# Edge selectors made from SBUF a batch ahead, and range sums turned one batch later, in a graph layer on one core

## Chip, cores and metric

One core of one Trainium2 chip. The metric is the device time of one execution in microseconds (us); lower is better.

## The reference

One layer of a graph network over 12500 nodes and 400000 edges, in fp32. Edges are sorted by destination; half of the destinations lie in the first quarter of the nodes, so at the low end a node has many edges and at the high end few.

```python
h = relu(layernorm(x))                                   # (12500, 160): 64 scalars, 32 vectors of 3
y0, y1 = h[:, :64] @ W_l1_0, einsum(h[:, 64:], W_l1_1)   # by node
w = silu(edge_attr_16 @ fc_W1) @ fc_W2                   # by edge: w_a 64, w_b 64, w_c 32, w_d 32
ys0, ys1 = y0[src], y1[src]                              # a gather of 160 numbers an edge
mid0 = concat(w_a * ys0 * e0, w_d * dot(ys1, e1) / sqrt(3))
mid1 = concat((w_b * ys0) x e1, (w_c * e0) * ys1)        # e0, e1: the 4 numbers of edge_attr_4
z = scatter_add(mid, dst)                                # sum over the edges of a node
out = x + C_S * (h @ W_sc) + C_X * (z @ W_l2)            # each scaled by node_vec1
```

## The kernel before, in words

A first phase normalises the nodes, maps them and writes y to HBM (`y_d`). The main loop then takes the 3125 tiles of 128 edges in 782 batches of four. An edge's contribution is not made out in full: VectorE makes 320 products an edge (weights times gathered row, `pr`), and the sum over edges comes from one fp32 matmul a tile, `selector^T @ pr`. The selector (`sel`) has 4 x 32 columns an edge: for each of a 32-node window it holds the edge's four e numbers where the edge ends at that node, and zero elsewhere. It is made in two steps: `own` compares a row 0..31 (`iota`) with the edge's node inside the window, and `sel` multiplies `own` by the four e numbers.

`ev` in SBUF holds five numbers an edge, the four e and the node inside the window, for a block of 96 tiles (24 batches). Before the change, ScalarE copies the batch's 20 columns of `ev` into PSUM, behind the batch's weights in the tile `pw` (`scale`, L524), and `own` (L620) and `sel` (L622) read them there.

A run of tiles that shares one 32-node window is a range. It has 24 tiles at the crowded end and 12, 8, 6, 4 and at last 3 at the other (`WTS`); 598 ranges in all, and four of them are a group. The matmuls of a range add up in one PSUM buffer `pz` (L636, two buffers). After the last one VectorE turns the sums by 32x32 blocks out of PSUM into `za` (L642, L643). Once a group is done, TensorE maps `za` by the output weights (`linear`, L649), places the rows (`add`, L661), and VectorE adds them to the result in SBUF (`accumulate`, L672).

The order on every engine is the one that the program writes (a manual schedule). In step b of the loop:

- TensorE: `weigh(b + 2)`, the weights of a later batch (L606, PSUM tile `pw`, two buffers, so it needs the products of batch b to be done); `linear` and `add` of the last group; then `sums(b)` (L636); every four steps two hidden layers (L585).
- VectorE: `products(b + 1)`, that is own (L620), sel (L622) and three multiplications (L529 and twice L533) that read `pw` and the gathered rows `yg`; then `accumulate` and some smaller work; then, inside `sums(b)`, the two turnings L642 and L643 of each range that ended in batch b.
- ScalarE: the copy L524 behind each `weigh`, and the activations.
- GpSimd: the gathers of rows (L571, an indirect DMA a tile), up to four batches ahead; a gather waits for the sums of the batch four before it ("rows keep step with the sums"). Sixteen batches get their rows from TensorE instead, without gathers.
- SyncE: loads of edge data.

`sel` has four buffers, `pr` three, `yg` six. At L720 and L723 sixteen times a pair of masks is made by VectorE from two SBUF tensors; L778 scales e numbers of those sixteen batches in place.

Of the kernel before, what the change touches and what calls it, by code (L numbers as in the profile page):

```python
# [10 lines left out]
F32 = mybir.dt.float32  # L11
I32 = mybir.dt.int32
AF = mybir.ActivationFunctionType
ALU = mybir.AluOpType
# [4 lines left out]
P = 128  # L19
M0 = 64  # L20
M1 = 32
D = M0 + 3 * M1
FC_IN = 16
FC_H = 64
NW = 2 * M0 + 2 * M1
PC = 320
ZC = 448
ZK = 5
GT = 4
BT = 32  # L30
WN = 32
# [20 lines left out]
def kernel(  # L52
# [19 lines left out]
    nc = tc.nc  # L72
# [7 lines left out]
    wts_of = [next(w for w in WTS if w == WTS[-1] or 2 * w * min((q + 1) * BLK, T) * N <= FILL * T * T)  # L80
              for q in range(NQ)]
    gstart, glist = [], []
    for q, w in enumerate(wts_of):
        gstart.append(len(glist))
        n = min(BLK, T - q * BLK)
# [3 lines left out]
    NB = (T + GT - 1) // GT  # L89
# [11 lines left out]
    iota = const.tile([P, 2 * P], F32, name="iota")  # L101
# [213 lines left out]
    def store(g, n, eng):  # L315
        node_dma(g, n, lambda rows, t, p: eng.dma_start(by_tile(out[rows, :]), acc[:p, g + t.start:g + t.stop, :]))
# [202 lines left out]
    before.close()  # L519


    def scale(pw, ev, n):

        nc.scalar.activation(pw[:, :n, NW:NW + 5], ev[:, :n, :], AF.Copy)  # L524

    def multiply(pr, wt, yg, n):

        y1 = yg[:, :n, M0:].rearrange("p t (c u) -> p t c u", c=3)
# [7 lines left out]
    with (  # L536
# [10 lines left out]
        hids, rows, wts, sels, z_ps, zT, o_sb, prs, sums_ps, summed = ({} for _ in range(10))  # L547
# [3 lines left out]
        group_of = [g for g, (_, _, n) in enumerate(glist) for _ in range(-(-n // GT))]  # L551
        first_of = [lo // GT for _, lo, _ in glist]
        assert len(group_of) == NB

        def tiles_of(b):
            return list(range(b * GT, min((b + 1) * GT, T)))

        def slots_of(b):
            n = len(tiles_of(b))
            return n if n == 1 else GT  # L560
# [38 lines left out]
        def weigh(b):  # L599
            hT = hids[b // 2]  # L600
            pw = p_w.tile([P, GT, 256], F32, name="pw")
            n = slots_of(b)
            for k in (0, 2, 1, 3):
                if k < n:
                    r, o = slice(FC_H * (k // 2), FC_H * (k // 2 + 1)), P * (b % 2 * 2 + k % 2)
                    nc.tensor.matmul(pw[:, k, 0:NW], hT[r, o:o + P], w2[r, :], start=True, stop=True)  # L606
            scale(pw, e4_of(b), n)
            wts[b] = pw

        def e4_of(b):  # L610
            o = b * GT % BLK
            return ev4[b * GT // BLK][0][:, o:o + GT, :]

        def products(b):

            n, wt, yg = slots_of(b), wts.pop(b), rows.pop(b)
            own = selp.tile([P, GT, WN], F32, name="own")
            sel = sels[b] = selp.tile([P, GT, 4, WN], F32, name="sel")[:, :n, :, :]
            pr = prs[b] = prod.tile([P, GT, PC], F32, name="pr")
            nc.vector.tensor_tensor(own[:, :n, :], iota[:, 0:WN].unsqueeze(1).to_broadcast([P, n, WN]),  # L620
                                    wt[:, :n, NW + 4:NW + 5].to_broadcast([P, n, WN]), ALU.is_equal)
            nc.vector.tensor_tensor(sel, own[:, :n, :].unsqueeze(2).to_broadcast([P, n, 4, WN]),  # L622
                                    wt[:, :n, NW:NW + 4].unsqueeze(3).to_broadcast([P, n, 4, WN]), ALU.mult)
            multiply(pr, wt, yg, n)

        def sums(b):
            pr, sel, g = prs.pop(b), sels.pop(b), group_of[b]
            q, lo, _ = glist[g]
            WT = wts_of[q]
            for k, t in enumerate(tiles_of(b)):  # L630
                w, o = divmod(t - lo, WT)
                if o == 0:
                    z_ps[g, w] = p_z.tile([P, 512], F32, name="pz")
                pz = z_ps[g, w]
                last = o == WT - 1 or t == T - 1
                mm = nc.tensor.matmul(pz[:, 0:PC], sel[:, slot(t), :, :], pr[:, slot(t), :], start=o == 0, stop=last)  # L636
                (halves if k == 1 else summed)[b] = mm.ins.name
                if last:
                    if w == 0:
                        zT[g] = post.tile([P, ZK, P], F32, name="za")  # L640
                    pz, at_w = z_ps.pop((g, w)), slice(WN * w, WN * (w + 1))
                    nc.vector.transpose(zT[g][:, :, at_w], pz[:, D:PC].rearrange("p (k u) -> p k u", k=ZK))  # L642
                    nc.vector.transpose(zT[g][0:32, :, at_w], pz[0:32, 0:D].rearrange("p (k u) -> p k u", k=ZK))  # L643

        def linear(g):
            m, za = WN * windows_of(g), zT.pop(g)
# [144 lines left out]
        weigh(0)  # L791
        if NB > 1:
            weigh(1)
        products(0)
        early = [x for x in groups if x[0] < LOW]
        assert early[-1][0] + early[-1][1] == LOW and first_of[GE] + K + len(early) <= NB
        for b in range(NB):
            g = group_of[b]
            k = b - first_of[g]
            if b + EARLY < NB:  # L800
                features(b + EARLY)
            q, r = divmod(b, KB)
            if r == 0:
                e4_load(q + 1)
            if r == KB - 4:
                e4_join(q + 1)
            u, v = divmod(b, SB)
            su, sv = divmod(b - SS, SK)
            if b + 2 < NB:
                weigh(b + 2)  # L810
            if g and 0 < k < K:
                (linear, add)[k - 1](g - 1)
            if b == SS - 8:
                skip_load(0)
            if sv in skips and 0 <= su < NU:
                skips[sv](su)
            low_pt = None
            if r == KB - 13 and q + 1 < NQ:
                low_pt = p_x.tile([MW, P], F32, name="px")[:windows_in(q + 1), :]
                turn_low(q + 1, low_pt)  # L820
            if r == KB - 11 and q + 1 < NQ:
                spread(q + 1, p_x.tile([P, MW], F32, name="px")[:, :windows_in(q + 1)])
            picked = None
            if u < XB:
                if v == 2:
                    hot_turn(u)
                elif v in (3, 6):
                    picked = look_up(u, HN * (v == 6))
                elif v == 7:
                    x_center(u)  # L830
                elif v in (9, 10):
                    x_turn(u, HN * (v == 10))
                elif v == 11:
                    x_map(u, 0)
            if v == 1 and 0 < u <= XB:
                x_map(u - 1, HN)
            if b + 1 < NB:
                products(b + 1)
            if g and k == K - 1:
                accumulate(g - 1)  # L840
            if sv == 7 and 0 <= su < NU:
                skip_add(su)
            if picked is not None:
                pick(u, HN * (v == 6), *picked)
            if v == SB - 2 and u < XB:
                x_scale(u)
            if v == 11 and u + 1 < XB:
                hot(u + 1)
            if r == KB - 15 and q + 1 < NQ:
                lowest(q + 1)  # L850
            if low_pt is not None:
                most(q + 1, low_pt)
            if r == KB - 8 and q + 1 < NQ:
                relate(rp, q + 1)
                if q + 2 == NQ:
                    any_far(rp, p_x.tile([1, 1], F32, name="px"))
            if early and b > first_of[GE] + K - 1:
                store(*early.pop(0), nc.sync)
            sums(b)
            for m, part in ((b + AHEAD - 1, slice(2, GT)), (b + AHEAD, slice(0, 2))):  # L860
                if AHEAD <= m < NB and m not in xs_of:
                    gather(m, part)
            if b % 4 == 0 and b + 4 < NB:
                hidden_pair((b + 4) // 2)
        assert SS + NU * SK <= first_of[GE] + K and NQ > 1
        for h in ([NG - 2] if NG > 1 else []) + [NG - 1]:
            for k, stage in enumerate((linear, add, accumulate)):
                if h == NG - 1 or min(k + 1, K - 1) > NB - 1 - first_of[NG - 1]:
                    stage(h)
# [5 lines left out]
    with (  # L875
# [4 lines left out]
        n = nc.values_load(far_i[0:1, 0:1], min_val=0, max_val=1)  # L880
        with tc.For_i(0, n, 1) as _:
# [8 lines left out]
            with tc.For_i(0, TP // GT, 1) as g:  # L890
# [4 lines left out]
                ev = fp.tile([P, GT, 5], F32, name="f_ev")  # L895
# [21 lines left out]
                pw = fpw.tile([P, GT, 256], F32, name="f_pw")  # L917
# [5 lines left out]
                for k in range(GT):  # L923
                    pd = fpp.tile([P, P], F32, name="f_pd")
                    nc.tensor.transpose(pd, df[:, k:k + 1].to_broadcast([P, P]), ident)
                    sel = fp.tile([P, P], F32, name="f_sel")
# [6 lines left out]
                                         scale=ev[:, k, 0:1])  # L933
                    nc.scalar.activation(ones[:, :, 0, :], low[:, M0:].rearrange("p (c u) -> p c u", c=3), AF.Copy,
                                         scale=ev[:, k, 0:1])
                    for c in range(3):
# [3 lines left out]
                                             scale=ev[:, k, 1 + c:2 + c])  # L940
# [10 lines left out]
                    pz = fpp.tile([P, ZC], F32, name="f_pz")  # L951
# [6 lines left out]
            with tc.For_i(0, NT, 1) as i:  # L958
# [4 lines left out]
                for c in range(3):  # L963
                    o = 256 + 64 * c
# [62 lines left out]
```

## Time and profile before

| | |
|---|---|
| runs | 4689.0 us median of 3 (4669.65 to 4695.63) |
| profiled execution | 4669.59 us, span 4667.7 us from the first instruction to the last |
| mean granted TensorE clock | 0.885 of full speed |
| busy | TensorE 80%, weight loads 53%, VectorE 59%, ScalarE 12%, GpSimd 63% |
| DMA | 329 MB, mean 70 GB/s |

The lines that follow come from one profiled execution. A group row has the line, the engine (PE TensorE, PEld its weight loads, DVE VectorE, ACT ScalarE, POOL GpSimd), the operation, out<-in, the shapes and the count; then busy us in all and mean ns of one; then the idle time of that engine just before these instructions, and what ended most of it ("issue": nothing that the profile shows). An fp32 matmul stands as two entries. A timeline row has start, duration, engine, line and operation, and in brackets the idle time before it and what ended it. Ends of matmuls are modelled.

### The profile page before, as it was taken

How to read it: one execution, taken by the hardware profiler on the slowest of the kernel's cores; microseconds unless marked ns; L12 is line 12 of the kernel's file. 1: busy time of each engine (PE TensorE's matmuls, PEld its weight loads, DVE VectorE, ACT ScalarE, POOL GpSimd, SP SyncE). 2: the span in 40 equal slices, each digit the busy share in tenths (PEclk: the TensorE clock that was granted, in tenths of full speed). 3: DMA queues.
4: the chain of work that ended last, by engine and by line, in shares of the span. 5: the costliest groups of instructions: out<-in, count | busy, mean ns of one | idle time of the engine just before them, and what ended most of it. 6: DMA issues, size and time to landing. Idle time of an engine off the chain costs nothing.

```text
span 4667.7 us, 53917 instructions
## 1 busy us (share of the span) xinstructions
PE 3717.5 (80%) x17202; PEld 2479.6 (53%) x17202; DVE 2735.8 (59%) x6877; ACT 580.9 (12%) x1845; POOL 2963.4 (63%) x3144
## 2 busy tenths in 40 slices
PE   7787787788877877777887788777877788888877
PEld 7455455455555554554555555555555555555545
DVE  5455555565556555555556566656556666666665
ACT  5111111111111101011101001111011110111100
POOL 5666666666666666666666666666666666666665
PEclk8888988889889888888888888988888898899998
DMA  7222222222222222222222222222222222222223
GB/s 192 69 61 64 64 65 66 65 65 64 62 64 65 69 72 62 67 69 66 68 68 67 65 71 67 68 67 67 65 70 66 68 63 64 68 67 71 63 63 113
DMA packets 262501, 329.03 MB, mean 70 GB/s; under 512 B 82888, under 2 KB 212216, under 8 KB 262216
## 3 DMA queue, kind: packets, MB, share of 16 engines
q0 software_dynamic: 150128, 256.23, 20.6%
q1 hardware_dynamic: 111590, 69.02, 5.2%
q8 instruction: 140, 2.29, 0.2%
q14 instruction: 145, 1.19, 0.1%
q10 hardware_dynamic: 498, 0.30, 0.0%
HBM read 307.67 MB, written 17.61 MB: 70 GB/s over the span
## 4 chain that ended last, share of the span: by engine, by line
PE 60%; another core or an unknown queue 13%; DVE 12%; issue 9%; ACT 2%; POOL 1%; DVEq 1%; ACTq 0%; DMA 0%; SPq 0%; POOLq 0%
PE pz L636 31%; PE pw L606 13%; PE px L649 6%; DVE pr L533 4%; PE px L585 3%; DVE pr L529 2%; PE px L661 2%; DVE za L642 1%; DVE za L643 1%; ACT hT L590 1%; POOL yg L571 1%; DVE own L620 1%; PE px L707 1%; PE px L706 1%
## 5 line engine op out<-in xcount | busy, mean ns | idle before, releaser
L571 POOL DMA_INDIRECT yg<-y_d,src_q x3061 | 2897.7, 947 | 1642.4 <-issue 803.1
L636 PE MATMUL pz<-pr,sel 128*128 128x320 f32 x6250 | 2069.0, 478 | 61.7 <-DVE za L643 39.6
L636 PEld LDWEIGHTS pz<-pr,sel 128*128 128x128 f32 x6250 | 1254.8, 211 | 607.6 <-issue 248.8
L606 PE MATMUL pw<-w,hT 64*128 64x192 f32 x6250 | 782.2, 368 | 508.3 <-DVE pr L533 276.0
L606 PEld LDWEIGHTS pw<-w,hT 64*128 64x128 f32 x6250 | 538.7, 198 | 953.3 <-issue 792.2
L642 DVE STREAM_TRANSPOSE za<-pz 128x160 f32<-128x160 f32 x598 | 205.5, 344 | 1034.8 <-PE pz L636 438.5
L533 DVE TENSOR_TENSOR pr<-pw,yg 128x384 f32<-128x384 f32 x1532 | 774.0, 547 | 0.0
L529 DVE TENSOR_TENSOR pr<-pw,yg 128x512 f32<-128x512 f32 x766 | 524.1, 684 | 192.5 <-DMA yg<-y_d,src_q 177.8
L622 DVE TENSOR_TENSOR sel<-own,pw 128x512 f32<-128x512 f32 x782 | 537.0, 687 | 27.0
L524 ACT ACTIVATE pw<-ev 128x20 f32<-128x20 f32 x782 | 149.5, 191 | 2957.7 <-PE pw L606 972.2
L649 PE MATMUL px<-wo,za 128*128 128x160 f32 x1500 | 330.7, 384 | 178.5 <-ACT hT L590 149.6
L649 PEld LDWEIGHTS px<-wo,za 128*128 128x128 f32 x1500 | 284.6, 247 | 220.1 <-ACT hT L590 165.0
L620 DVE TENSOR_TENSOR own<-iota,pw 128x128 f32<-128x128 f32 x782 | 199.6, 255 | 247.6 <-ACT pw L524 209.4
L585 PE MATMUL px<-xe,w 32*128 32x512 f32 x782 | 270.3, 658 | 63.0 <-ACT os L651 33.6
L590 ACT ACTIVATE hT<-px 128x512 f32<-128x512 f32 x391 | 220.2, 594 | 554.9 <-PE px L585 173.9
L643 DVE STREAM_TRANSPOSE za<-pz 32x160 f32<-32x160 f32 x598 | 202.2, 338 | 20.5
L672 DVE SCALAR_TENSOR_TENSOR acc<-px,a_sb,acc 128x160 f32 x300 | 114.1, 380 | 120.0 <-remote 33.6
L585 PEld LDWEIGHTS px<-xe,w 32*128 32x128 f32 x782 | 72.4, 189 | 177.7 <-issue 99.1
L661 PE MATMUL px<-os,place 128*128 128x160 f32 x600 | 133.3, 349 | 35.8 <-ACT os L651 24.2
L661 PEld LDWEIGHTS px<-os,place 128*128 128x128 f32 x600 | 94.1, 205 | 76.1 <-issue 41.7
L715 DVE SCALAR_TENSOR_TENSOR acc<-px,look,acc 128x160 f32<-128x160 f32 x98 | 33.1, 379 | 131.2 <-PE pz L636 38.3
L651 ACT ACTIVATE os<-px 128x160 f32<-128x160 f32 x150 | 44.9, 300 | 349.5 <-PE pz L636 91.2
(128 smaller groups left out, 1435.0 us busy)
## 6 DMA issues: line engine op xcount, KB each, us to landing
yg<-y_d,src_q POOLq DMA_INDIRECT x3061
xe<-in_e SPq DMA_DIRECT2D x784, 32.0 KB
xs<-in_x SPq DMA_DIRECT2D x48, 160.0 KB
acc<-in_x SPq DMA_DIRECT2D x11, 640.0 KB
y_d<-ys SPq DMA_DIRECT2D x11, 640.0 KB
out<-acc SPq DMA_DIRECT2D x11, 640.0 KB
raw<-in_e SPq DMA_DIRECT2D x32, 192.0 KB
src_q<-in_src SPq DMA_DIRECT2D x32, 48.0 KB
```

What stands on the lines that cost most here:

```text
L529: nc.vector.tensor_mul(pr[:, :n, :].rearrange("p t (x u) -> p t x u", x=2)[:, :, :, 0:M0], wt[:, :n, 0:NW].rearrange("p t (x u) -> p t x u ...
L533: nc.vector.tensor_mul(pr[:, :n, D * x + M0:D * (x + 1)].rearrange("p t (c u) -> p t c u", c=3), wt[:, :n, 96 * x + M0:96 * (x + 1)].unsqu ...
L571: fetch = nc.gpsimd.indirect_dma_start(out=yg[:, slot(t), :], out_offset=None, in_=y_d, in_offset=bass.IndirectOffsetOnAxis(ap=ev4[t // BL ...
L585: nc.tensor.matmul(ph, w1[r, :], xe[r, :], start=True, stop=True)
L590: nc.scalar.activation(hT, ph, AF.Silu, scale=1.0 / math.sqrt(FC_IN))
L606: nc.tensor.matmul(pw[:, k, 0:NW], hT[r, o:o + P], w2[r, :], start=True, stop=True)
L622: nc.vector.tensor_tensor(sel, own[:, :n, :].unsqueeze(2).to_broadcast([P, n, 4, WN]), wt[:, :n, NW:NW + 4].unsqueeze(3).to_broadcast([P, ...
L636: mm = nc.tensor.matmul(pz[:, 0:PC], sel[:, slot(t), :, :], pr[:, slot(t), :], start=o == 0, stop=last)
L642: nc.vector.transpose(zT[g][:, :, at_w], pz[:, D:PC].rearrange("p (k u) -> p k u", k=ZK))
L643: nc.vector.transpose(zT[g][0:32, :, at_w], pz[0:32, 0:D].rearrange("p (k u) -> p k u", k=ZK))
L649: nc.tensor.matmul(po[:m, :], za[:, k, :m], wo[:, k, :], start=k == 0, stop=k == ZK - 1)
L661: nc.tensor.matmul(ps[:, h, :], place[:m, h, :], os[:m, :], start=True, stop=True)
```

## The change

`scale` and its call go. A new `select(b)` makes own and sel from `ev` in SBUF; it is called for b + 2 behind `products(b + 1)`, so the selector is there a batch earlier and stands behind the products in VectorE's queue instead of before them. `own` lies in another pool, with two buffers. The turning moves out of `sums` into `leave_ranges`, which works off a list of ended ranges: it is called in step b before `sums(b)`, so that ranges that ended in batch b - 1 are turned behind `products(b + 1)` and `select(b + 2)`. Where the range after the next one starts by batch b + 1 at the latest, its PSUM buffer is wanted sooner, and the ranges are turned at once as before.

```diff
-    def scale(pw, ev, n):
-        nc.scalar.activation(pw[:, :n, NW:NW + 5], ev[:, :n, :], AF.Copy)
...
+        starts = [lo + o for q, lo, n in glist for o in range(0, n, wts_of[q])]
+        ended = []
...
-            scale(pw, e4_of(b), n)
             wts[b] = pw
...
+        def select(b):
+            n, ev = slots_of(b), e4_of(b)
+            own = post.tile([P, GT, WN], F32, name="own")
+            sel = sels[b] = selp.tile([P, GT, 4, WN], F32, name="sel")[:, :n, :, :]
+            nc.vector.tensor_tensor(own[:, :n, :], iota[:, 0:WN].unsqueeze(1).to_broadcast([P, n, WN]),
+                                    ev[:, :n, 4:5].to_broadcast([P, n, WN]), ALU.is_equal)
+            nc.vector.tensor_tensor(sel, own[:, :n, :].unsqueeze(2).to_broadcast([P, n, 4, WN]),
+                                    ev[:, :n, 0:4].unsqueeze(3).to_broadcast([P, n, 4, WN]), ALU.mult)
+
         def products(b):
             n, wt, yg = slots_of(b), wts.pop(b), rows.pop(b)
-            own = selp.tile([P, GT, WN], F32, name="own")
-            sel = sels[b] = selp.tile([P, GT, 4, WN], F32, name="sel")[:, :n, :, :]
             pr = prs[b] = prod.tile([P, GT, PC], F32, name="pr")
-            nc.vector.tensor_tensor(own[:, :n, :], iota[:, 0:WN].unsqueeze(1).to_broadcast([P, n, WN]),
-                                    wt[:, :n, NW + 4:NW + 5].to_broadcast([P, n, WN]), ALU.is_equal)
-            nc.vector.tensor_tensor(sel, own[:, :n, :].unsqueeze(2).to_broadcast([P, n, 4, WN]),
-                                    wt[:, :n, NW:NW + 4].unsqueeze(3).to_broadcast([P, n, 4, WN]), ALU.mult)
             multiply(pr, wt, yg, n)
...
                 if last:
-                    if w == 0:
-                        zT[g] = post.tile([P, ZK, P], F32, name="za")
-                    pz, at_w = z_ps.pop((g, w)), slice(WN * w, WN * (w + 1))
-                    nc.vector.transpose(zT[g][:, :, at_w], pz[:, D:PC].rearrange("p (k u) -> p k u", k=ZK))
-                    nc.vector.transpose(zT[g][0:32, :, at_w], pz[0:32, 0:D].rearrange("p (k u) -> p k u", k=ZK))
+                    ended.append((g, w))
+                    i = starts.index(lo + w * WT) + 2
+                    if i < len(starts) and starts[i] // GT <= b + 1:
+                        leave_ranges()
+
+        def leave_ranges():
+            while ended:
+                g, w = ended.pop(0)
+                if w == 0:
+                    zT[g] = post.tile([P, ZK, P], F32, name="za")
+                pz, at_w = z_ps.pop((g, w)), slice(WN * w, WN * (w + 1))
+                nc.vector.transpose(zT[g][:, :, at_w], pz[:, D:PC].rearrange("p (k u) -> p k u", k=ZK))
+                nc.vector.transpose(zT[g][0:32, :, at_w], pz[0:32, 0:D].rearrange("p (k u) -> p k u", k=ZK))
...
+        select(0)
         products(0)
+        if NB > 1:
+            select(1)
...
             if b + 1 < NB:
                 products(b + 1)
+            if b + 2 < NB:
+                select(b + 2)
             if g and k == K - 1:
                 accumulate(g - 1)
...
+            leave_ranges()
             sums(b)
...
+        leave_ranges()
         for h in ([NG - 2] if NG > 1 else []) + [NG - 1]:
```

## The prediction

> **What bounds the kernel now.** I read the page's busy line and clock row, then its groups, the waits, and one stretch of the timeline. The main loop has 782 batches of four edge tiles; the span less the 116 us before the first gather is 4552 us, 5.8 us a batch.
>
> ```profile
> span 4667.7 us, 53917 instructions
> PE 3717.5 (80%) x17202; PEld 2479.6 (53%) x17202; DVE 2735.8 (59%) x6877; ACT 580.9 (12%) x1845; POOL 2963.4 (63%) x3144
> PEclk8888988889889888888888888988888898899998
> L571 POOL DMA_INDIRECT yg<-y_d,src_q x3061 | 2897.7, 947 | 1642.4 <-issue 803.1
> L571 POOL DMA_INDIRECT yg<-y_d,src_q x3061: 940/946/1370, 116.1 to 4643.8; - x192
> L636 PE MATMUL pz<-pr,sel 128*128 128x320 f32 x6250 | 2069.0, 478 | 61.7 <-DVE za L643 39.6
> L606 PE MATMUL pw<-w,hT 64*128 64x192 f32 x6250 | 782.2, 368 | 508.3 <-DVE pr L533 276.0
> L642 DVE STREAM_TRANSPOSE za<-pz 128x160 f32<-128x160 f32 x598 | 205.5, 344 | 1034.8 <-PE pz L636 438.5
> L643 DVE STREAM_TRANSPOSE za<-pz 32x160 f32<-32x160 f32 x598 | 202.2, 338 | 20.5
> L533 DVE TENSOR_TENSOR pr<-pw,yg 128x384 f32<-128x384 f32 x1532 | 774.0, 547 | 0.0
> L529 DVE TENSOR_TENSOR pr<-pw,yg 128x512 f32<-128x512 f32 x766 | 524.1, 684 | 192.5 <-DMA yg<-y_d,src_q 177.8
> L622 DVE TENSOR_TENSOR sel<-own,pw 128x512 f32<-128x512 f32 x782 | 537.0, 687 | 27.0
> L524 ACT ACTIVATE pw<-ev 128x20 f32<-128x20 f32 x782 | 149.5, 191 | 2957.7 <-PE pw L606 972.2
> L620 DVE TENSOR_TENSOR own<-iota,pw 128x128 f32<-128x128 f32 x782 | 199.6, 255 | 247.6 <-ACT pw L524 209.4
> L649 PE MATMUL px<-wo,za 128*128 128x160 f32 x1500 | 330.7, 384 | 178.5 <-ACT hT L590 149.6
> ```
>
> No engine is full. VectorE is busy 59%, and its largest idle time, 1034.8 us, stands in front of L642, the turning of a range's sums: it waits there for TensorE. TensorE's largest idle time, 508.3 us, stands in front of L606, the weights of a later batch, and the releaser named first is VectorE's products. So the two wait for each other in turn. The timeline shows how:
>
> ```profile
> 1015.70 2.05 PE L636 MATMUL pz<-pr,sel 128*128 128x320 f32 x7
> 1017.17 0.17 DVE L778 TENSOR_TENSOR ev<-ev,val 128x16 f32<-128x16 f32 x1
> 1017.68 0.92 PE L606 MATMUL pw<-w,hT 64*128 64x192 f32 x8
> 1018.53 2.42 PE L636 MATMUL pz<-pr,sel 128*128 128x320 f32 x8
> 1019.32 0.35 DVE L642 STREAM_TRANSPOSE za<-pz 128x160 f32<-128x160 f32 x1 [1.99 <-PE pw L606]
> 1019.46 0.19 ACT L524 ACTIVATE pw<-ev 128x20 f32<-128x20 f32 x1 [4.21 <-PE pw L606]
> 1019.71 0.34 DVE L643 STREAM_TRANSPOSE za<-pz 32x160 f32<-32x160 f32 x1
> 1019.98 0.24 DVE L620 TENSOR_TENSOR own<-iota,pw 128x128 f32<-128x128 f32 x1
> 1020.25 0.69 DVE L622 TENSOR_TENSOR sel<-own,pw 128x512 f32<-128x512 f32 x1
> 1020.75 0.94 POOL L571 DMA_INDIRECT yg<-y_d,src_q  x1 [0.30 <-issue]
> 1020.86 0.68 DVE L529 TENSOR_TENSOR pr<-pw,yg 128x512 f32<-128x512 f32 x1
> 1021.46 1.01 DVE L533 TENSOR_TENSOR pr<-pw,yg 128x384 f32<-128x384 f32 x2
> 1022.00 0.95 POOL L571 DMA_INDIRECT yg<-y_d,src_q  x1 [0.30 <-issue]
> 1022.61 0.92 PE L606 MATMUL pw<-w,hT 64*128 64x192 f32 x8 [1.66 <-DVE pr L533]
> ```
>
> VectorE is done at 1017.34 and stands still until 1019.32 for news of the sums. Only then come turning, own, selector and products, 3.15 us up to 1022.47, and TensorE, done with its own work at 1020.95, waits 1.66 us. The products that it waited for needed nothing of what stood before them in the queue.
>
> The second resource is GpSimd. Back to back its gathers start 1.25 us apart (1020.75 and 1022.00), so 3061 of them need 3826 us, 84% of the loop; with the 116 us before and about 25 us behind, the program cannot end before 3967 us while a gather costs this.
>
> **The change part by part.**
>
> *The copy L524 goes.* 782 x 191 ns of ScalarE, 12% busy: worth nothing in itself. What counts is that own (L620) no longer waits for it, 209.4 us. That wait lies in the same chain as the next item, so I don't add it.
>
> *Own and selector move behind the products, one batch ahead; turning moves behind the next batch's products and selector.* Together these took up to 0.34 + 0.34 + 0.26 + 0.69 = 1.63 us (as the starts lie, 1.54 us: 1019.32 to 1020.86) and the wait in front of them out of the path from "sums ended" to "products done". For what TensorE gets back, I walked the batches in the trace. In 305 of them L606 begins within 0.35 us after the end of the products that free its PSUM buffer, with TensorE idle before it: 503 us in all, of the row's 508.3, 1.65 us each. For each I asked how much earlier those products could have begun: not before the copy behind their weights ran (a stand-in for "weights ready"), not before 2.4 us after their last gather was issued (the shortest distance with which the trace shows products to follow), not before the end of the previous products plus 0.95 us for the selector. The smaller of that advance and the wait comes to 376 us, three quarters. Bounds: three quarters of the 276.0 us that the row puts on the products by name is 207 us; the whole row is 508.
>
> ```profile
> L215 DVE TENSOR_SCALAR at<-off,node_of 32x6 f32<-32x6 f32 x36 | 8.4, 233 | 0.7
> L215 DVE TENSOR_SCALAR at<-off,node_of 32x8 f32<-32x8 f32 x24 | 5.5, 228 | 0.5
> ```
>
> *Short ranges.* L215 runs four times for each block of 24 batches, with as many columns as the block has groups: 9 blocks have 6 groups (ranges of four tiles, 216 batches), 6 have 8 (three tiles, 144 batches, and 14 of the last block). With three tiles the condition on the next-but-one range is always met, so turning stays where it was and still waits for the sums; but own and selector are already done then, so 0.95 us of the path goes. Ranges of four tiles are one batch each: their turning now ends 1.6 us after products that the same sums need anyhow, against 0.85 us of weights in between on TensorE. Where VectorE is the late one this gives back up to 0.8 us in those 216 batches, 170 us at worst; where it is early, nothing. Since the products come earlier by more than that in the example (1.98 us of standing still), I take nothing and keep 170 us for the upper end.
>
> *The final map L649* needs the last range's turning, now a step later and behind 0.95 us of selector. 150 groups; today 178.5 us of idle stand before it, put on ScalarE's hT. Between -100 (half of that goes as VectorE is earlier) and +120 (150 x 0.8); I take zero, as weights of 0.85 us still lie in between.
>
> *VectorE's own durations.* Selector and own now read two SBUF tensors and no PSUM. Such operations are in the trace:
>
> ```profile
> L720 DVE TENSOR_TENSOR oh<-iota,xp 128x512 f32<-128x512 f32 x16 | 10.9, 681 | 0.0
> L723 DVE TENSOR_TENSOR mask<-iota,xt 128x392 f32<-128x392 f32 x16 | 8.9, 558 | 0.0
> L233 DVE TENSOR_TENSOR over<-drel,off 128x96 f32<-128x96 f32 x32 | 8.2, 258 | 1.1
> 1264.09 0.68 DVE L720 TENSOR_TENSOR oh<-iota,xp 128x512 f32<-128x512 f32 x1
> 1264.30 1.29 POOL L571 DMA_INDIRECT yg<-y_d,src_q  x1 [0.30 <-issue]
> 1264.69 0.56 DVE L723 TENSOR_TENSOR mask<-iota,xt 128x392 f32<-128x392 f32 x1
> 1265.90 0.94 POOL L571 DMA_INDIRECT yg<-y_d,src_q  x1 [0.30 <-issue]
> ```
>
> 681 against 687 ns: no difference. But L720 and L723 also read two SBUF tensors, and the gather issued under them took 1.29 us in place of 0.95. All 23 gathers that such an operation touches fit one rule within 5 ns on average: 0.12 us after its start a gather reads, and if a two-SBUF operation runs then, the gather is held until that operation ends (1264.30 + 0.12 to 1264.77 is 0.35 us; seen 0.34). The present own and selector, each with one operand in PSUM, hold nothing: 0.95 us is the gathers' mean.
>
> *So the change puts a price on gathers.* Laid over the present times of own and selector, the reading point of 572 of the 3061 gathers falls into one of them, 128 us of holding in all, at most 0.68 us for one. I charge all of it, since POOL after the gain would be at (3826 + 128) / 4300 = 92% of the loop and has little left to hide it in. Bounds: zero if it is absorbed in the 840 us that POOL now idles beyond issue (1642.4 - 803.1); 0.67 us in each of the 766 gathered batches, 513 us, if selector and gather fall into step.
>
> [...]
>
> *Waits added.* select(b+2) writes a four-deep buffer last read by sums(b-2); the products queued before it need the same sums for their three-deep buffer. No new wait. No DMA is added or moved, and nothing changes on SP.
>
> *Sum.* The profiled execution took 4669.6 us, 0.4% under the median of 4689.0. 4669.6 - 376 + 128 = 4422 us; by the same 0.4% the median comes to 4440 us.
>
> **The rivals.**
>
> *Lock-step with the gathers (slower).* Products wait for a gather's landing, the selector follows them at a fixed distance, and the gathers run at a fixed pitch; if that puts one reading point into every selector, POOL pays 0.67 us a batch: 4669.6 - 376 + 513 = 4807, as median 4827 us. It turns from gain to loss at 376 / 766 = 0.49 us a batch. For: GpSimd is the next limit, and only 177.8 us of today's waits are on landing because others are longer. Against: the pitch 1.25 us and the batch of 5.8 us are no multiples, and the present phases give 128 / 766 = 0.17 us.
>
> *The late news stays (little gain).* In the example sums that began at 1015.70 ended by TensorE's own record near 1017.7, yet VectorE and ScalarE learn of that TensorE work at 1019.32 and 1019.46. If such lateness, not the queue's order, is what starves TensorE, the products still wait for the weights' late news, and only half comes back: 4669.6 - 188 + 128 = 4610, as median 4629 us.
>
> *The clock recovers too (larger gain).* The granted clock is in tenths 8 to 9 throughout, on one core; if it falls because TensorE idles, fewer waits bring it up. TensorE's whole 508 us of waits at L606 and the lower bound of POOL's price give 4669.6 - 508 + 0 = 4162; with 90 us of POOL's price 4252, as median 4270. POOL's floor of 3967 us allows it. [...]
>
> *The change does nothing* would need the copy and the turning to be off the path, against the 1.66 us wait above; it is in the second rival's upper part.
>
> **How the numbers follow.** My forecast 0.50, lock-step 0.18, late news 0.20, recovered clock 0.12. The range 4240 to 4780 us takes in the last at its 4270, the forecast with its bounds (207 us of gain and 170 us of late turning: 4669.6 - 207 + 128 + 170 = 4761, as median 4781) and late news; lock-step's main part lies outside, and a tail below. Faster by over 0.5%, about what a measurement of this kernel can tell: 0.48 of the forecast, 0.12, and 0.14 of late news: 0.74. Within 0.5%: 0.06 of late news. Slower: 0.20, lock-step and 0.02 of the forecast at its worst bounds.
>
> **What would show it.** Right: L642's idle falls from 1034.8 to well under 500 us; idle before L606 from 508.3 to under 250; no own waits for ACT; own and sel keep 255 and 687 ns; gathers' mean rises from 947 to about 990 ns (128 / 3061 = 42 ns). Wrong: a mean gather over 1.07 us (0.49 us a batch / 4), which is lock-step; idle before L606 still about 500 with products waiting for weights, which is late news; or more idle before L636 with za named, the price of late turning.

## The result and the profile after

| | before | after |
|---|---|---|
| median | 4673.01 us (4661.4 to 4695.63, 19 runs) | 4703.01 us (4686.17 to 4718.5, 19 runs) |
| profiled execution | 4669.59 us, span 4667.7 | 4704.88 us, span 4703.1 |
| mean granted clock | 0.885 | 0.871 |

The ratio is 1.0057 [1.0046, 1.0067]: 0.6% slower, small but clear of the spread of the runs, where 4440 us was forecast. The experiments ran on four chips of two kinds, told apart by the kernel before: about 4673 us at a granted clock of 0.885, as in the table, on the one, and 3967 to 3971 us at 0.97 on the other. They are called the slower and the faster chip here, and every ratio is against the kernel before on the same chip.

The page of the kernel after, its span, busy line, clock row and groups:

```profile
span 4703.1 us, 52886 instructions
PE 3717.8 (79%) x17202; PEld 2490.8 (53%) x17202; DVE 2769.7 (59%) x6877; ACT 449.8 (10%) x1063; POOL 3037.1 (65%) x3144
PEclk8888888889888888888888888888888898888888
L569 POOL DMA_INDIRECT yg<-y_d,src_q x3061 | 2971.0, 971 | 1605.9 <-issue 766.1
L637 PE MATMUL pz<-pr,sel 128*128 128x320 f32 x6250 | 2064.8, 477 | 103.8 <-DVE za L653 62.0
L525 DVE TENSOR_TENSOR pr<-pw,yg 128x512 f32<-128x512 f32 x766 | 520.6, 680 | 1147.7 <-DMA yg<-y_d,src_q 638.0
L604 PE MATMUL pw<-w,hT 64*128 64x192 f32 x6250 | 767.3, 364 | 243.3 <-DVE pr L529 113.3
L659 PE MATMUL px<-wo,za 128*128 128x160 f32 x1500 | 343.6, 395 | 341.0 <-ACT hT L588 224.6
L618 DVE TENSOR_TENSOR sel<-own,ev 128x512 f32<-128x512 f32 x782 | 541.7, 693 | 30.8 <-DVE own L616 2.7
L652 DVE STREAM_TRANSPOSE za<-pz 128x160 f32<-128x160 f32 x598 | 204.2, 341 | 249.1 <-PE pz L637 109.6
L616 DVE TENSOR_TENSOR own<-iota,ev 128x128 f32<-128x128 f32 x782 | 219.4, 281 | 0.5 <-ACT ev L389 0.5
```

The waits that were to go are gone: turning (L652) stands idle for 249.1 us where it was 1034.8, the weights (L604) for 243.3 where it was 508.3, and own waits for nothing (it takes 281 ns where it took 255, 20 us in all). But VectorE now waits at the first products (L525), 1147.7 us where it was 192.5, mostly for rows to land (638.0 against 177.8). TensorE's idle time in all, span less busy, went from 4667.7 - 3717.5 = 950 to 4703.1 - 3717.8 = 985 us: what left L604 stands at L659 (178.5 to 341.0), L637 (61.7 to 103.8) and smaller lines.

The rows come from GpSimd, and its row carries the difference. The gathers got 2971.0 - 2897.7 = 73.3 us longer in all, and the idle time before them shrank by 1642.4 - 1605.9 = 36.5 us; the difference of 36.8 is that of the spans, 35.4. As a sum this must come out, since GpSimd hardly does anything else (2971.0 of its 3037.1 us of work are these gathers). What it tells is which of the two moved, and the experiments are read by it. Of the idle time, about 940 us is the 0.30 us behind each gather (the gathers that wait for nothing, below, have 939.6); the rest, 703 us before and 666 after, is waiting, above all for sums:

```profile
POOL yg L569 <- PE pz L637: 328.8, 193, 8.6
POOL yg L569 <- remote: 299.2, 145, 3.1
```

These are GpSimd's waits after (us in total, times, longest). "remote" means that the profile found no instruction that had ended at that moment. A stretch of the timeline after shows both the held gather and such news:

```profile
2001.14 0.28 DVE L616 TENSOR_TENSOR own<-iota,ev 128x128 f32<-128x128 f32 x1
2001.46 0.69 DVE L618 TENSOR_TENSOR sel<-own,ev 128x512 f32<-128x512 f32 x1
2001.73 1.24 POOL L569 DMA_INDIRECT yg<-y_d,src_q  x1 [0.30 <-issue]
2002.07 0.34 DVE L652 STREAM_TRANSPOSE za<-pz 128x160 f32<-128x160 f32 x1
...
2004.64 0.69 DVE L525 TENSOR_TENSOR pr<-pw,yg 128x512 f32<-128x512 f32 x1 [1.56 <-DMA yg<-y_d,src_q]
...
2008.32 0.19 PEld L637 LDWEIGHTS pz<-pr,sel 128*128 128x128 f32 x1 [0.53 <-issue]
...
2009.04 0.19 PEld L637 LDWEIGHTS pz<-pr,sel 128*128 128x128 f32 x1 [0.53 <-issue]
...
2009.65 0.18 PEld L604 LDWEIGHTS pw<-w,hT 64*128 64x128 f32 x1 [0.43 <-issue]
...
2012.66 0.30 ACT L661 ACTIVATE os<-px 128x160 f32<-128x160 f32 x1 [14.93 <-remote]
2012.75 0.68 DVE L725 SCALAR_TENSOR_TENSOR acc<-px,look,acc 128x160 f32<-128x160 f32 x2 [5.57 <-remote]
...
2013.05 0.94 POOL L569 DMA_INDIRECT yg<-y_d,src_q  x1 [2.54 <-remote]
```

By the rule that the prediction fitted to 23 gathers of the trace before, the gather at 2001.73 reads 0.12 us later, at 2001.85, inside the selector that ends at 2002.15: 0.30 us, and it took 1.24 in place of 0.95. From 2008.32 TensorE's weight loads come one by one, and from 2011.13 two by two, 0.6 to 0.8 us apart, and ScalarE, VectorE and GpSimd all hear of finished work within 0.4 us of each other, at 2012.66 to 2013.05.

### The profile page after: what moved, and what is told of

Read it like the earlier page. It is cut to its first block, busy times and chain, and to the rows that moved or that the text cites. A ratio compares the mean times of both kernels' runs of the same rounds, so it can differ in the third digit from the quotient of the medians.

```text
span 4703.1 us, 52886 instructions
## 1 busy us (share of the span) xinstructions
PE 3717.8 (79%) x17202; PEld 2490.8 (53%) x17202; DVE 2769.7 (59%) x6877; ACT 449.8 (10%) x1063; POOL 3037.1 (65%) x3144
## 4 chain that ended last, share of the span: by engine, by line
PE 41%; another core or an unknown queue 31%; issue 11%; DVE 10%; ACT 2%; DMA 1%; POOL 1%; DVEq 0%; ACTq 0%; SPq 0%; POOLq 0%
PE pz L637 21%; PE pw L604 7%; PE px L659 6%; DVE pr L529 3%; PE px L583 2%; DVE pr L525 2%; PE px L671 2%; DVE sel L618 2%; ACT hT L588 1%; POOL yg L569 1%; DVE za L652 1%; DVE own L616 1%; DMA yg<-y_d,src_q 1%; DVE za L653 0%
## 5 line engine op out<-in xcount | busy, mean ns | idle before, releaser
L569 POOL DMA_INDIRECT yg<-y_d,src_q x3061 | 2971.0, 971 | 1605.9 <-issue 766.1
L637 PE MATMUL pz<-pr,sel 128*128 128x320 f32 x6250 | 2064.8, 477 | 103.8 <-DVE za L653 62.0
L637 PEld LDWEIGHTS pz<-pr,sel 128*128 128x128 f32 x6250 | 1254.2, 210 | 645.5 <-issue 285.5
L525 DVE TENSOR_TENSOR pr<-pw,yg 128x512 f32<-128x512 f32 x766 | 520.6, 680 | 1147.7 <-DMA yg<-y_d,src_q 638.0
L604 PE MATMUL pw<-w,hT 64*128 64x192 f32 x6250 | 767.3, 364 | 243.3 <-DVE pr L529 113.3
L604 PEld LDWEIGHTS pw<-w,hT 64*128 64x128 f32 x6250 | 526.2, 196 | 684.7 <-issue 464.2
L659 PE MATMUL px<-wo,za 128*128 128x160 f32 x1500 | 343.6, 395 | 341.0 <-ACT hT L588 224.6
L618 DVE TENSOR_TENSOR sel<-own,ev 128x512 f32<-128x512 f32 x782 | 541.7, 693 | 30.8 <-DVE own L616 2.7
L659 PEld LDWEIGHTS px<-wo,za 128*128 128x128 f32 x1500 | 296.9, 257 | 382.5 <-ACT hT L588 263.8
L652 DVE STREAM_TRANSPOSE za<-pz 128x160 f32<-128x160 f32 x598 | 204.2, 341 | 249.1 <-PE pz L637 109.6
L616 DVE TENSOR_TENSOR own<-iota,ev 128x128 f32<-128x128 f32 x782 | 219.4, 281 | 0.5 <-ACT ev L389 0.5
L347 POOL DMA_INDIRECT xr<-in_x,xi x64 | 61.2, 956 | 37.4 <-issue 14.4
```

What stands on the lines that cost most here:

```text
L525: nc.vector.tensor_mul(pr[:, :n, :].rearrange("p t (x u) -> p t x u", x=2)[:, :, :, 0:M0], wt[:, :n, 0:NW].rearrange("p t (x u) -> p t x u ...
L569: fetch = nc.gpsimd.indirect_dma_start(out=yg[:, slot(t), :], out_offset=None, in_=y_d, in_offset=bass.IndirectOffsetOnAxis(ap=ev4[t // BL ...
L659: nc.tensor.matmul(po[:m, :], za[:, k, :m], wo[:, k, :], start=k == 0, stop=k == ZK - 1)
```

## The experiments

### The loop without gathers

```diff
...
-            for k, t in list(enumerate(tiles_of(b)))[part]:
+            for k, t in list(enumerate(tiles_of(b)))[part] if b < 6 else []:
...
```

> The kernel before without the gathers of batches 6 and later (the products read rows of the first six batches, so the sums are of other rows). Theory G, the loop of gathers and sums sets the time of both kernels: about 4000 us or less, and TensorE's idle time before the weights under 150 us. Theory P, TensorE's own late completions set it: over 4500 us, and the completions of its weights still reach ScalarE several us late.

> The changed kernel without the gathers of batches 6 and later (the sums are of other rows). Theory G: under 4000 us, and below the kernel before without gathers by about the 376 us that the prediction had, since nothing takes them up any more. Theory P: over 4500 us and equal to the other within 1%.

On the faster chip: 3328.1 us from before, ratio 0.8384 [0.8367, 0.8401], and 3295.6 from after, 0.8302 [0.8286, 0.8319]. The groups of the first and then of the second:

```profile
L609 PE MATMUL pw<-w,hT 64*128 64x192 f32 x6250 | 721.6, 349 | 55.2 <-DVE pr L533 40.7 <-ACT hT L593 4.5
```

```profile
L607 PE MATMUL pw<-w,hT 64*128 64x192 f32 x6250 | 722.5, 350 | 13.0 <-DVE pr L529 8.9 <-ACT hT L591 4.0
```

Without gathers the change does what the forecast had it do: TensorE's wait before the weights goes from 55.2 to 13.0 us, and the time falls by 32 us, 1%. The mechanism exists, and it is small: most of the 508.3 us of that wait isn't there once the gathers are out (57.1 us remain on the slower chip, below).

The kernel before without gathers was run again, on the faster chip and on the slower:

> The kernel before without the gathers of batches 6 and later (the sums are of other rows). On a chip with the granted clock 0.885: if TensorE is late by itself, the time stays over 4200 us and the clock under 0.92; if it is late only beside the gathers, 3330 us and a clock of 0.99, as on the other chips.

> The kernel before without the gathers of batches 6 and later (the sums are of other rows). On a chip with the granted clock 0.885: over 4200 us if TensorE is late by itself, 3330 us if it is late only beside gathers. On the others 3327 us, as before.

3326.3 us (0.8385 [0.8369, 0.84]) and 3349.6 us (0.7171 [0.7147, 0.7196]). The slower chip's page:

```profile
PE 3243.4 (97%) x17202; PEld 2186.5 (65%) x17202; DVE 2704.2 (81%) x6877; ACT 571.0 (17%) x1845; POOL 88.7 (3%) x107
PEclk8899999999999999999999999999999999999999
```

So in the main loop the slower chip is hardly slower by itself: without gathers TensorE is 97% busy there too, its mean clock is 0.990, and of the 23 us against the faster chip 19 lie ahead of the loop (its first hidden layer is activated at 115.8 us, against 96.5). Its wait before the weights is 57.1 us, as on the faster chip. What makes the slower chip 700 us slower shows only where gathers run beside TensorE.

### The loop without "rows keep step with the sums"

```diff
-                if of is not None:
+                if False:
                     tc.add_manual_dep(fetch.ins, of,
```

> The kernel before without the rule that a gather waits for the sums four batches before it; only the six row buffers hold gathers back. Theory G: GpSimd's 840 us of waits beyond issue fall under 400 us and the time falls to 4300 to 4500 us. Theory P: the time stays within 1% of 4670 us, for the products wait for TensorE in place of rows.

> The changed kernel without that rule. Theory G: products no longer wait 638 us for landings, GpSimd is nearly full, 4150 to 4400 us. Theory P: within 1% of 4700 us.

> The kernel before without the rule that a gather waits for the sums four batches before. On a chip with the clock 0.885: if the loop of gathers and late sums sets the time, GpSimd's 700 us of waits fall under 300 and the time under 4400 us; if TensorE's lateness alone sets it, the time stays within 1% of 4673 us. On the others 3951 us, as before.

On the faster chip, from before: 3951.3 us, 0.9952 [0.9936, 0.9969], and again 3952.1, 0.9963 [0.995, 0.9976]; from after: 4050.0 us, 1.0201 [1.0184, 1.0218]. The gathers of before and then of after, from the groups of GpSimd:

```profile
L571 POOL DMA_INDIRECT yg<-y_d,src_q x3061 | 2901.2, 948 | 939.6 <-issue 848.8 <-DVE own L620 23.5 <-DVE za L642 19.2
```

```profile
L569 POOL DMA_INDIRECT yg<-y_d,src_q x3061 | 2999.5, 980 | 939.7 <-issue 833.2 <-DVE za L652 41.7 <-DMA yg<-y_d,src_q 14.9
```

Here GpSimd waits for nothing, and it alone sets the end: its first gather starts at 98.9 us and its last at 3931.4, 1.252 us a gather. Under that limit selectors from SBUF cost what they add to the gathers: 2999.5 - 2901.2 = 98 us, and the times differ by 99; the new order on VectorE costs nothing beside it. Without the rule the kernel before gets faster by 0.4 to 0.5%. All three runs fell on the faster chip, so the figures that the expectations have for the slower one stay untested.

### The parts of the change, on the faster chip

The kernel after as it is; selectors a batch ahead with their operands still in PSUM (the copy is made a batch earlier, into spare columns of `pw`); selectors from SBUF at the old place; and before with late turning alone.

> The changed kernel itself, beside the others. In the runs so far the kernel before takes 3971 us where TensorE is granted 0.97 of its clock, and its gathers back to back set that. Theory H, the selectors hold the gathers and GpSimd passes that on in full: 4045 to 4070 us (a gather's mean of 971 to 980 ns in place of 948, 3061 times), 1.9 to 2.5% slower. Theory O, the new order on VectorE costs the time: about the same, but then without the gathers getting longer to explain it.

```diff
...
-            n, ev = slots_of(b), e4_of(b)
+            n, ev = slots_of(b), copies.pop(b)
...
```

> The changed order in full, but ScalarE copies the five numbers a batch earlier into the spare columns of the weights' PSUM tile and the selectors read them there, so no selector has two SBUF inputs. Theory H: gathers back at 948 ns, the time within 0.5% of before or a little under it. Theory O: slower by about as much as the changed kernel.

```diff
-            scale(pw, e4_of(b), n)
...
-                                    wt[:, :n, NW + 4:NW + 5].to_broadcast([P, n, WN]), ALU.is_equal)
+                                    ev[:, :n, 4:5].to_broadcast([P, n, WN]), ALU.is_equal)
...
```

> The kernel before, with own and sel at their old place but made from SBUF, without ScalarE's copy. Theory H: as slow as the changed kernel or slower, 1.9 to 3%, with gathers of 971 to 985 ns. Theory O: within 0.5% of before.

```diff
...
+            leave_ranges()
             sums(b)
...
```

> The kernel before with the late turning alone; selectors are made from PSUM at their old place. Theory H: gathers stay at 948 ns and the time within 0.5% of before. Theory O: slower by 1 to 2%.

> The kernel before with late turning alone. On a chip with the clock 0.885: if late turning is what costs the changed kernel its 0.6%, 20 to 40 us over before; if it costs only together with the early selector, within 10 us of before. On the others 26 us over before, as measured.

| | us | ratio | gathers in all, us | waits, us |
|---|---|---|---|---|
| after | 4098.7 | 1.0331 [1.0317, 1.0345] | 2995.8 | 56 |
| a batch ahead from PSUM, late turning | 4019.6 | 1.0128 [1.0112, 1.0144] | 2895.7 | 79 |
| from SBUF at the old place | 4030.2 | 1.0155 [1.0141, 1.0169] | 2969.2 | 18 |
| late turning alone | 3992.9 | 1.0069 [1.0055, 1.0082] | 2902.5 | 37 |
| late turning alone, again | 3991.3 | 1.0060 [1.0046, 1.0073] | | |

The waits are the idle time of the gathers' row less the 939.6 us above. The rows, in the order of the table:

```profile
L569 POOL DMA_INDIRECT yg<-y_d,src_q x3061 | 2995.8, 979 | 995.4 <-issue 697.3 <-PE pz L637 114.6 <-DMA yg<-y_d,src_q 75.6
```

```profile
L570 POOL DMA_INDIRECT yg<-y_d,src_q x3061 | 2895.7, 946 | 1018.4 <-issue 733.0 <-PE pz L646 160.9 <-PE pw L605 38.1
```

```profile
L571 POOL DMA_INDIRECT yg<-y_d,src_q x3061 | 2969.2, 970 | 957.2 <-issue 684.1 <-PE pz L635 73.0 <-DMA yg<-y_d,src_q 28.0
```

```profile
L573 POOL DMA_INDIRECT yg<-y_d,src_q x3061 | 2902.5, 948 | 976.2 <-issue 672.4 <-PE pz L638 96.2 <-DVE za L654 46.0
```

Selectors that read only SBUF lengthen the gathers, by 100 us in the new order (2995.8 against 2895.7) and by 68 at the old place (2969.2 against 2901.2 in the kernel before without the step rule); read from PSUM they lengthen nothing (946 and 948 ns), wherever they stand. At the old place they cost 61 us of time (0.0155 x 3967), and late turning alone costs 24 to 27. Of the 131 us of the whole change (0.0331 x 3967) that leaves 43 to 46, which come only when both stand together with the selector a batch ahead.

The second row of the table doesn't split them cleanly. Its copies for the next batch lie in the weights' tile, so that the weights now wait for the selector:

```profile
L605 PE MATMUL pw<-w,hT 64*128 64x192 f32 x6250 | 732.3, 351 | 461.9 <-DVE sel L627 403.5
```

In the kernel after, the same wait is 346.8 us, put on the products. So the 51 us of that row (0.0128 x 3967) may hold a cost of this wait beside that of the order, and the 79 us by which it is faster than after need not be the holding alone; no run tells them apart. That the order costs through the step rule shows in the kernel after without it: 4050.0 us, 49 less than with it, and GpSimd's 56 us of waits are gone.

Neither theory had the sizes. H, the holding, asked for at most 4070 us for the kernel after, at least 1.9% for selectors from SBUF at the old place, and times within 0.5% of before wherever selectors read PSUM; 4099 us, 1.6%, and 1.3 and 0.6 to 0.7% were measured. O, the order, asked that the third kernel be within 0.5%, and it is 1.6% slower.

How late turning costs is in TensorE's waits for turned sums (`za`), in the kernel after and with late turning alone:

```profile
PE pz L637 <- DVE za L653: 138.3, 135, 3.1
PE px L659 <- DVE za L653: 91.2, 66, 4.9
```

```profile
PE px L660 <- DVE za L654: 53.3, 14, 4.0
PE pz L638 <- DVE za L654: 36.8, 66, 2.8
```

Turning stands behind products that wait for a landing; until it is done the sums of the next-but-one range have no buffer and the final map no operand.

### The same on the slower chip

The kernel before again, with a profile; the kernel after with turning put back into `sums`; the selector multiplied twice, in after and in the version that reads PSUM.

> The kernel before, for a profile beside the others. Where TensorE is granted 0.97 of its clock: 3967 us, gathers of 948 ns, GpSimd's waits beyond its own pitch of 1.25 us under 30 us in all. Should this chip be like that of the first runs (clock 0.885): 4670 us, with about 700 us of such waits.

```diff
...
-                    ended.append((g, w))
...
+                    nc.vector.transpose(zT[g][:, :, at_w], pz[:, D:PC].rearrange("p (k u) -> p k u", k=ZK))
...
```

> The changed kernel, but with every range turned at once inside the sums as before; selectors still a batch ahead and from SBUF. If late turning costs what it cost alone (26 us) the time is 4070 us, 2.6% over before; if it is late turning and the early selector together that make the order's 53 us, 4045 us. The holding of the gathers, about 79 us, stays in both.

> The changed kernel with every range turned at once. On a chip with the clock 0.97: before plus the holding (79 us) and, if the early selector costs nothing by itself, nothing more, 4046 us; if late turning costs only its 26 us, 4073 us. With the clock 0.885: 4668 us, as measured.

```diff
+            nc.vector.tensor_tensor(sel, own[:, :n, :].unsqueeze(2).to_broadcast([P, n, 4, WN]),
+                                    ev[:, :n, 0:4].unsqueeze(3).to_broadcast([P, n, 4, WN]), ALU.mult)
```

> The changed kernel with sel made twice in a row, which doubles the larger of the two operations that hold gathers. Theory H: gathers' mean rises by a further 20 to 27 ns over the 979, and the time by 60 to 90 us over the changed kernel's 4099. If instead the time on VectorE itself costs, the next kernel rises as much.

> The changed kernel with sel made twice. On a chip with the clock 0.97, holding paid in full: gathers' mean 991 to 1005 ns and 4140 to 4190 us, that is the rise of the mean times 3061 over the changed kernel's 4099 us. With the clock 0.885: 4702 us, as measured.

> The same doubling where the selectors are read from PSUM: as much more work for VectorE (0.69 us a batch) but no second SBUF input. Theory H: gathers stay at 946 to 948 ns and the time rises by under 30 us over the 4020 of that kernel with sel made once.

| | us | ratio | gathers in all, us | waits, us |
|---|---|---|---|---|
| before | 4673.0 | 1.0016 [0.9998, 1.0033] | 2899.2 | 700 |
| a batch ahead from SBUF, turned at once | 4668.3 | 0.9989 [0.9975, 1.0004] | 2990.7 | 606 |
| the same, again | 4670.9 | 1.0001 [0.9985, 1.0017] | | |
| after, selector twice | 4701.9 | 1.0071 [1.0049, 1.0094] | 3034.3 | 597 |
| the same, again | 4702.4 | 1.0059 [1.0031, 1.0087] | | |
| a batch ahead from PSUM, late turning, selector twice | 4697.6 | 1.0057 [1.0037, 1.0078] | 2898.4 | 715 |

The gathers of the second, the fourth and the sixth line:

```profile
L568 POOL DMA_INDIRECT yg<-y_d,src_q x3061 | 2990.7, 977 | 1545.4 <-issue 778.5 <-remote 292.8 <-PE pz L636 267.8
```

```profile
L569 POOL DMA_INDIRECT yg<-y_d,src_q x3061 | 3034.3, 991 | 1536.1 <-issue 793.2 <-PE pz L639 278.4 <-remote 247.9
```

```profile
L570 POOL DMA_INDIRECT yg<-y_d,src_q x3061 | 2898.4, 947 | 1654.5 <-issue 777.8 <-PE pz L648 321.5 <-remote 227.2
```

Beside these, the two kernels of the table and the loop without gathers, nothing was run on the slower chip; where an expectation here has figures for the faster one, they stay untested.

Holding costs next to nothing here. With the selector made a second time the gathers of the kernel after get 3034.3 - 2971.0 = 63 us longer, and its time stays: 4702 us against 4703, 1.0071 and 1.0059 against 1.0057. GpSimd waits 597 us in place of 666 instead. (With selectors from PSUM the gathers are 136 us shorter in all and the ratio is 1.0057 too; but there the weights wait for the selector as above, so that pair differs in more than the holding.) The early selector and its holding together come to nothing (0.9989 and 1.0001). What is left is late turning: the three kernels with it lie 0.6 to 0.7% up, the one without it, run on two chips, at 1.00; 1.0057 less 1.0001, or less 0.9989, is 26 to 32 us. All of these have the selector a batch ahead; late turning alone wasn't run on the slower chip.

Where the early selector's gain went is in the groups of VectorE, then of TensorE, with turning at once:

```profile
L525 DVE TENSOR_TENSOR pr<-pw,yg 128x512 f32<-128x512 f32 x766 | 510.5, 666 | 558.3 <-DMA yg<-y_d,src_q 363.7 <-remote 85.5 <-PE pz L636 44.3
L642 DVE STREAM_TRANSPOSE za<-pz 128x160 f32<-128x160 f32 x598 | 205.9, 344 | 974.8 <-PE pz L636 435.8 <-remote 320.8 <-issue 87.7
```

```profile
L603 PE MATMUL pw<-w,hT 64*128 64x192 f32 x6250 | 774.9, 365 | 343.1 <-DVE pr L529 205.6 <-issue 98.6 <-ACT hT L587 15.3
```

TensorE's wait before the weights falls from 508.3 us (483.4 in the kernel before on this very chip) to 343.1, and VectorE's wait for landings rises from 177.8 (191.2) to 363.7; the time is unchanged.

## Why the prediction was wrong

**376 us regained before the weights: the step that failed.** The local part was right: idle before L642 fell to 249.1 us (asked for: well under 500), before L604 to 243.3 (under 250), own waits no more for the copy. The time didn't follow. The walk let products begin earlier while it held every landing at its old time, and took what TensorE no longer waited at one line as time saved. But a gather is issued only after sums four batches back have been heard of, the products need its rows, and the sums need the products. The landings did not stay: the gathers got 73.3 us longer in all and their waits fell by only 36.5. With turning at once on the same kind of chip the gain was 0 (0.9989 and 1.0001), and VectorE's wait had moved to the landing. The prediction had the row for it (177.8 us on landing, GpSimd at 84% of the loop) and used it only for the lock-step. No rival said that the same wait would come back at the landing with the time unchanged. (The walk itself, done again over the trace, gives 302 batches, 468 us of waits and 349 us of gain: three quarters as well, a little less in all.)

**128 us for held gathers: gathers are held, but the condition and the effect were wrong.** The rule of the reading point gives how long a gather is held (1.24 us at 2001.73), but not which ones are. A gather that begins before the selector, or up to some 0.045 us behind it, wasn't held, though it read inside it; from the timeline of the kernel after:

```profile
2058.59 0.77 DVE L618 TENSOR_TENSOR sel<-own,ev 128x512 f32<-128x512 f32 x1
2058.64 0.95 POOL L569 DMA_INDIRECT yg<-y_d,src_q  x1 [1.07 <-PE pw L604]
```

Here the gather takes its 0.95 us and the selector is the longer one, 0.77 us in place of 0.69. In this trace 429 gathers read inside a selector that has over 0.04 us left: the 47 that began at most 0.044 us behind its start were not held, the 382 that began 0.050 us or more behind it all were. On the faster chip it is 25 (up to 0.042) and 657 (from 0.046). The prediction couldn't see this: where gathers read inside L720 or L723, they began at least 0.129 us behind the start. With this condition the present times of own and selector give about 56 us in place of 128. The mean was asked for at about 990 ns and came to 971 on the slower chip and 979 on the faster, 73 and 100 us; that this lies as near to 128 as to 56 is luck, as the new order moved gathers and selectors against each other.

The effect was paid in full only where GpSimd had no wait to give up: all of it on the faster chip without the step rule (98 us of gathers, 99 of time), 61 of 68 with selectors at the old place, and none on the slower chip, where the lower bound, zero, was the value. That selectors made from SBUF lengthen gathers at all, which the step took from 23 gathers, was right: 979 ns a gather on the faster chip, against 946 with the operands in PSUM.

**Late turning, taken at zero.** It cost 24 to 27 us alone on the faster chip and 26 to 32 beside the early selector on the slower, inside the bound of 170, and there it decides the sign. The step reasoned that VectorE is early, from one example. It is early only as long as it waits for sums; once it waits for rows, turning stands behind that wait. The sign named for it showed: idle before the sums 61.7 to 103.8 us, with za at 62.0.

**The final map, taken at zero.** Its idle time rose by 341.0 - 178.5 = 162 us, over the bound of 120. Of the rise 75 us are put on ScalarE's hidden layer (224.6 after, 149.6 before) and 38 on `za`, where before there was none. With turning at once it is 212.1 and 199.2 us, so most of the rise comes with late turning; but with late turning and selectors from PSUM, made twice, it is 201.0. What it depends on stays open.

**GpSimd's floor of 3967 us.** Right as a method: without the step rule and with the first gather at 98.9 us in place of 116.1, 98.9 + 3826 + 25 = 3950, and 3951.3 was measured. (That before itself takes 3967 us on the faster chip is chance.) There the kernel before already lay within 16 us of this floor, so that there the change could hardly gain and its longer gathers had to show.

**The rivals.** Lock-step: no, 971 ns against its 1070. Late news: its sign, idle of about 500 us before the weights, didn't show, and 4629 us was not the time; yet late news is real on the slower chip. From the start of a hidden layer's second matmul entry to its activation, a mean over 391 pairs of them, 3.46 us pass before and 4.35 after; on the faster chip, in the kernel after, it is 1.15, and on the slower without gathers 1.20. Recovered clock: no, it fell from 0.885 to 0.871, as TensorE's idle time grew from 950 to 985 us. On this kind of chip the clock was 0.871 at 79% busy, 0.885 at 80% and 0.990 at 97% without gathers; that idling is the cause is not shown.

**Own and selector's durations.** The selector kept its time (693 against 687 ns); own didn't, 281 against 255. It is 276 also from PSUM a batch ahead, and 259 from SBUF at the old place, so the longer time goes with the new place in VectorE's queue and not with the operands.

**What stays open.** Why TensorE's news is late on the slower chip once gathers run. That the loop of sums, gathers and products sets the pace there is argued from the waits, not shown: the step rule was not taken out on that chip, nor was late turning alone tried, nor early selectors from PSUM with turning at once, nor after without gathers. On the faster chip no run has the early selector without late turning.

## What to carry to other kernels

A wait that vanishes at one instruction is no gain until the loop that it belongs to has been followed round (here the 508.3 us before the weights fell to 243.3, and the time rose by 0.6%): ask of each wait removed what its engine waits for next, and whether that thing starts any earlier. Where one engine issues all the transfers, write its account first, durations plus gaps plus waits: here 63 us of extra duration were free where it had over 600 us of waits to give up (4702 against 4703 us), and 98 us were paid in full, 99 us of time, where it had none. Work moved behind an operation that waits for a transfer inherits that wait, and so does everybody who needs its result: late turning cost 24 to 32 us here.

## What the hardware showed that I had not expected

The same program took 4673 us on one chip and 3967 on another, 18% apart, with the clock at 0.885 and 0.97, and without gathers 3350 and 3327. The sign on the slower one is that releases often can't be tied to the end of a matmul. ScalarE's largest wait in the kernel after, on the slower chip and then on the faster:

```profile
ACT hT L588 <- remote: 1586.8, 124, 26.7
```

```profile
ACT hT L588 <- PE px L583: 2288.3, 213, 21.5
```

A selector that reads only SBUF held a gather only where the gather began later than the selector, by 0.046 us or more: all 1039 such gathers, of the 1111 counted above in two traces, and none of the other 72. Where the two began nearly at once it was the selector that took longer, 0.71 to 0.77 us in place of 0.69: 15 of the 47 others in the kernel after on the slower chip, with the gather 0.011 us ahead to 0.044 us behind.

A verdict on a change can thus differ in size from chip to chip, here 0.6% against 3.3%: on the faster one GpSimd has next to no waits left to give up (56 us in the kernel after), on the slower one 666.
